# Sorting two entries of one layer per round, with the longest tile split by count

## The chip, the cores and the metric

The kernel runs on one core of a Trainium2 chip. The metric is the device time of one execution in microseconds, the median of several runs. A core has five engines that work through their own instruction streams side by side: TensorE (PE, matrix products), VectorE (DVE, elementwise work), ScalarE (ACT, functions and copies), GpSimd (POOL, which here issues the gathering DMAs) and SyncE (SP, which issues plain DMAs). They wait for each other through semaphores.

## What is computed

The input is a batch of 16 graphs of 1024 nodes, with 64 features per node and a sparse weighted adjacency matrix. Four layers follow each other. Layers 0 and 1 are products with the adjacency and small dense products. Layers 2 and 3 replace the sum over the neighbours by quantiles:

```
# layer 0: x = layernorm(x + tanh([x, adj @ x] @ W1 + b1) @ W2 + b2)
# layer 1: x = layernorm(x + (adj / max(rowsum(adj), 1)) @ x)
# layers 2 and 3, each with its own W1, b1, W2, b2:
adj_ = adjacency with ones on the diagonal
neigh = adj_ > 0, without the diagonal
# from a node with more than 10 neighbours every skip-th neighbour is taken out,
# skip = (neighbours + 1) // 2, and each taken edge goes in both directions
nd = adj_ after that > 0
s = sort(where(nd, x[neighbour], inf))       # per node and feature, over the neighbours
agg = sum over tau, w in (0.25, 0.25), (0.5, 0.5), (0.75, 0.25):
      w * (linear interpolation of s at tau * (count - 1))
x = layernorm(x + (relu((x + agg) @ W1 + b1) @ W2 + b2) * mask)
```

The set of valid neighbours is the same for layers 2 and 3, so a graph's lists are made once and used twice.

## The kernel before

**Words.** An entry is one of the 16 graphs. Below, "layer 0" and "layer 1" of the sorting are the reference's layers 2 and 3; this is also how the code counts them. A slot is one neighbour position of a list: 64 features (elements) for each of 128 rows.

**Preparing an entry.** `features` loads the adjacency in 128-column pieces, computes the first two layers, and keeps a 0/1 matrix of who is near whom. `lists` thins the neighbours, orders the rows of the graph by their count of neighbours, and writes for each ordered tile of 128 rows the list of neighbour indices (`idx`); VectorE's MAX8 finds them eight at a time. `ordered` brings features, masks and counts into the same order, and makes the interpolation weights. The lists of one entry are made after those of the one before.

**Tiles.** The 1024 ordered rows are 8 tiles of 128 rows, and tile t has at most `SIZES[t]` neighbours per row: 10, 11, 13, 14, 15, 17, 19 and 33. For the first seven, called the listed tiles here, GpSimd gathers the neighbours' features from a table in HBM: one indirect DMA for each slot but the first (L362), 92 for an entry and a layer, into a ring of 60 slots (`got_s`) that holds two entries side by side. For the tile of 33 slots, called the tail, no lists are made: TensorE picks the rows with one-hot matrices (`hot`), 24 products for each slot (L358), and ScalarE copies them out of PSUM (L742).

**Sorting.** A fixed network of min and max operations between strided views, alternating between the tile and a second buffer `other`, leaves the wanted order statistics in place (`exchange_plan`). Each min or max is one VectorE instruction for both entries of a pair at once (all VectorE calls of this part show line L207, a helper that counts their cost). `weigh` multiplies the wanted slots by their weights on ScalarE (L781) and adds them up on VectorE, into `agg`. `finish` runs the small dense network and the layernorm, and scatters the result rows with eight indirect DMAs (L826): to the second table after layer 0, to the output after layer 1.

**Rounds.** Round k sorts layer 0 of entry k and layer 1 of entry k - 2 side by side, for k = 0 to 17. Rounds 0 and 1 therefore have layer 0 alone, rounds 16 and 17 layer 1 alone, and each other round has a pair. In a round the tiles go from 19 slots down to 10, then the tail. `finish_round` of a round is done during the next.

**Order.** On VectorE, ScalarE and TensorE the order is written by the program itself: `Weave` keeps a clock of estimated VectorE time, and after each exchange it lets every other piece of work (a Python generator that yields how long its step takes) advance to that clock. `fetch` issues a tile's gathers as soon as the ring has a place and the entries are ready, in the order of `order_of_tiles`. `prepare` may start entries up to `allowed`, that is k + 2. GpSimd's and SyncE's DMAs are placed by a scheduler.

Of the kernel before, what the change touches and what calls it, by code (L numbers as in the profile page):

```python
# [12 lines left out]
F32 = mybir.dt.float32  # L13
# [8 lines left out]
P = 128  # L22
# [3 lines left out]
SIZES = (10, 11, 13, 14, 15, 17, 19, 33)  # L26
LEAST = (1,) + SIZES[:-1]
KS = -(-(max(SIZES[:-1]) - 1) // 8) * 8
KW = max(SIZES)
HOTS = 6  # L30
# [182 lines left out]
def adj_resnorm_kernel(ctx: ExitStack, tc: tile.TileContext, x, adj_t, nodemask, w01, b01, w02, b02,  # L213
# [3 lines left out]
    NT = N // P  # L217
    H = w21.shape[1]
# [42 lines left out]
    bounds = const.tile([1, 2 * NT], F32, name="bounds")  # L261
    for t in range(NT):
        nc.vector.memset(bounds[:, t : t + 1], float(SIZES[t]))
        nc.vector.memset(bounds[:, NT + t : NT + t + 1], float(LEAST[t]))
# [39 lines left out]
    want_ids = const.tile([P, NT, most_wanted], F16, name="want_ids")  # L304
# [6 lines left out]
    weights = const.tile([P, NT, most_wanted], F32, name="weights")  # L311
    mask_all = const.tile([P, B, NT], F32, name="mask_all")
    with tc.tile_pool(name="setup", bufs=1) as setup, \
# [11 lines left out]
        n1 = setup.tile([P, NT], F32, name="n1s")  # L325
        nc.vector.tensor_scalar(n1, nth.to_broadcast([P, NT]), -1.0, None, op0=ALU.add)
        hats(weights, [P, NT, most_wanted], n1, want_ids)
# [8 lines left out]
    table = [[dram.tile([N + 1, C], F32, name=f"table{layer}{i}") for i in range(3)] for layer in range(2)]  # L336
# [69 lines left out]
    def features(b, e):  # L406
# [72 lines left out]
        nc.sync.dma_start(table[0][b % 3][:N, :].rearrange("(t p) c -> p t c", p=P), x2)  # L479
        while b >= 2 and not entries[b - 2].filled[0]:  # L480
            yield 2
        parts = s.feat.tile([P, NT, 3, C], BF, name="x2p")
# [3 lines left out]
    def lists(b, e, pace):  # L486
# [103 lines left out]

        order = s.sets.tile([P, NT, N], BF, name="order", tag="takes")
# [7 lines left out]
        e.idx = s.feat.tile([P, NT, KS], I32, name="idx", bufs=5)  # L599
        pks, codes, found = {}, {}, []  # L600
        for t in (*reversed(range(NT)), -1, -2, -3):
# [19 lines left out]
            if 0 <= done < NT - 1:  # L621
                best = s.work.tile([P, KS], F16, name="best", bufs=1)
                less = s.work.tile([P, N], F16, name="less", bufs=1)
                rest, size = codes[done], -(-(SIZES[done] - 1) // 8) * 8
                for k in range(0, size, 8):
                    dve.max(best[:, k : k + 8], rest)
                    if k + 8 < size:
                        dve.match_replace(less, best[:, k : k + 8], rest, 0.0)
                        rest = less
                dve.tensor_scalar(e.idx[:, done, :size], best[:, :size], -1.0, float(N), op0=ALU.mult, op1=ALU.add)  # L630
        e.listed = True

    def ordered(b, e, order, own):
# [17 lines left out]
        e.rows = s.feat.tile([P, NT], I32, name="rows", bufs=6)  # L651
        dve.tensor_copy(e.rows, sorted_own[:, :, 1])
        e.out_rows = s.feat.tile([P, NT], I32, name="out_rows", bufs=6)
        dve.tensor_scalar(e.out_rows, sorted_own[:, :, 1], float(b * N), None, op0=ALU.add)
        e.mask = s.feat.tile([P, NT], F32, name="mask_s", bufs=6)
        dve.tensor_copy(e.mask, sorted_own[:, :, 2])
        yield 7
        while b >= 3 and entries[b - 3].xs[1] is None:
            yield 2
        e.xs[0] = s.feat.tile([P, NT, C], F32, name="x2s", bufs=3)  # L660
# [9 lines left out]
        while b >= 4 and not entries[b - 4].filled[1]:  # L670
            yield 2
        place = s.feat.tile([P, NT, P], F16, name="place", bufs=4)
# [12 lines left out]

        e.none = s.feat.tile([KW - 1, P], BF, name="none", bufs=5)
        wts = s.feat.tile([P, NT, most_wanted], F32, name="wts", bufs=5)
        for h in range(NH):
# [11 lines left out]
            for q in range(G):  # L700
                nc.tensor.matmul(pw[:, q, :], counted[:, q, :], weights[:KW, h * G + q, :], start=True, stop=True)
            yield 9
            nc.scalar.copy(wts[:, half, :], pw)
# [9 lines left out]
        nc.tensor.transpose(pc[:1, :NT], ends[:, P - 1 : P], ident[:NT, :NT])  # L713
        nc.tensor.transpose(pc[:1, NT : 2 * NT], ends[:, 0:1], ident[:NT, :NT])
        yield 7
        mf = s.work.tile([1, 2 * NT + 1], F32, name="mf", bufs=1)
        nc.scalar.copy(mf[:, : 2 * NT], pc[:1, : 2 * NT])
        yield 5
        dve.tensor_sub(mf[:, : 2 * NT], mf[:, : 2 * NT], bounds)
        dve.tensor_scalar(mf[:, NT : 2 * NT], mf[:, NT : 2 * NT], -1.0, None, op0=ALU.mult)  # L720
        dve.reduce_max(mf[:, 2 * NT :], mf[:, : 2 * NT], axis=AX.X)
        dve.tensor_copy(over[:, b : b + 1], mf[:, 2 * NT :])

    def members(k):

        return [(m, b, entries[b]) for m, b in enumerate((k, k - 2)) if 0 <= b < B]

    def fill(k):

        while k and (k - 1, NT - 1) not in free:  # L730
            yield 1
        t = NT - 1
        size = SIZES[t]
        got = tails[k] = s.lists.tile([P, 2, size, C], F32, name="got", tag="got_l", bufs=1)
        for m, b, e in members(k):
            while e.parts[m] is None or e.xs[m] is None or e.place is None or e.none is None:
                yield 1
            nc.scalar.copy(got[:, m, 0, :], e.xs[m][:, t, :])
            waiting = None

            def empty():
                nc.scalar.copy(got[:, m, waiting[0] : waiting[0] + 4, :], waiting[1])  # L742

            for i in range(1, size):
# [13 lines left out]
                whole = i < LEAST[t]  # L758
# [3 lines left out]
                pick(pg[:, i - first, :], hot, e.parts[m], whole)  # L762
# [8 lines left out]
            e.filled[m] = True  # L771

    def weigh(k, t, got, agg, which):

        want = wants[t]
        while any(e.wts is None for m, b, e in members(k)):
            yield 1
        prods = got[:, :, : len(want), :]
        for i, slot_id in enumerate(want):
            for m, b, e in members(k):  # L780
                nc.scalar.activation(prods[:, m, i, :], got[:, m, slot_id, :], AF.Copy, scale=e.wts[:, t, i : i + 1])  # L781
            if i % 6 == 5:
                yield 3
        yield 13
        left = len(want)
        while left > 2:
            more = left // 2
            dve.tensor_add(prods[:, which, :more, :], prods[:, which, :more, :], prods[:, which, left - more : left, :])
            left -= more
        dve.tensor_add(agg[:, which, t, :], prods[:, which, 0, :], prods[:, which, 1, :])  # L790
        free.add((k, t))

    def finish(b, e, layer, agg):
# [3 lines left out]
        y = s.work.tile([P, NT, C], F32, name="y_m", bufs=1)  # L797
        dve.tensor_add(agg, agg, xc)
        yield 2
        for h in range(NH):  # L800
            pt = s.psum.tile([P, HALF], F32, name="pt", tag="m", bufs=1)
# [3 lines left out]
            o_t = s.work.tile([C, HALF], F32, name="o_t", bufs=1)  # L805
            nc.scalar.copy(o_t, pt[:C])
            yield 3
            ph = s.psum.tile([P, HALF], F32, name="ph", tag="m", bufs=1)
            nc.tensor.matmul(ph[:H], w1s, o_t, start=True, stop=True)  # L809
            yield 7  # L810
            h_t = s.work.tile([H, HALF], F32, name="h_t", tag="o_t", bufs=1)
            nc.scalar.activation(h_t, ph[:H], AF.Relu, bias=b1c)
            yield 3
            pd = s.psum.tile([P, G, C], F32, name="pd", tag="m", bufs=1)
# [6 lines left out]
        xn = agg if layer else s.feat.tile([P, NT, C], F32, name="x3s", bufs=3)  # L821
        yield from settle(xn, y, "m")
        yield 1
        dst, rows = (out_rows_of, e.out_rows) if layer else (table[1][b % 3], e.rows)
# [10 lines left out]
    def read_back(b, e, src):  # L835

        while b and not entries[b - 1].filled[1]:
            yield 2
# [3 lines left out]
        parts = s.feat.tile([P, NT, 3, C], BF, name="x3p", bufs=1)  # L842
# [3 lines left out]
    class Weave:  # L846
# [34 lines left out]
        def finish(self, gen):  # L881
            while self.runs(gen):
# [3 lines left out]
                               wts=None, parts=[None, None], xs=[None, None], filled=[False, False]) for _ in range(B)]  # L886
# [4 lines left out]
    order_of_tiles = [(k, t) for k in range(B + 2) for t in reversed(range(NT - 1))]  # L891
# [16 lines left out]
    def fetch(must=-1):  # L908

        while len(gots) < len(order_of_tiles):  # L910
            n = len(gots)
            k, t = order_of_tiles[n]
            first = room[0] if room[0] + SIZES[t] <= ROOM else 0
            taken = [i for i in holders[first : first + SIZES[t]] if i is not None and order_of_tiles[i] not in free]
            there = [e.xs[1] is not None if m else ready(b) for m, b, e in members(k)]
# [6 lines left out]
            for m, b, e in members(k):  # L922
                while not (e.xs[1] is not None if m else ready(b)):
                    weave.advance()
                nc.scalar.copy(got[:, m, 0, :], e.xs[m][:, t, :])
                for i in range(1, SIZES[t]):
                    gather(got[:, m, i, :], table[m][b % 3], e.idx[:, t, i - 1 : i])
            gots.append(got)

    def finish_round(k, agg, sums):  # L930
# [3 lines left out]
        for m, b, e in members(k):  # L934
            yield from finish(b, e, m, agg[:, m])

    def sort_round(k):
# [4 lines left out]
        first = members(k)[0][0]  # L942
        which = slice(first, first + len(members(k)))
        agg = s.feat.tile([P, 2, NT, C], F32, name="agg")
        sums = []
        for t in (*reversed(range(NT - 1)), NT - 1):
            if t == NT - 1:
                weave.finish(filling)
                got = tails[k]
            else:  # L950
                n = order_of_tiles.index((k, t))
                fetch(n)
                got = gots[n]
            other = s.lists.tile([P, 2, SIZES[t], C], F32, name="other", bufs=1)
            pair = got[:, which], other[:, which]
            for is_max, d, v, i, j, to in usual[t]:
# [319 lines left out]
```

## Time and profile before

| what | value |
|---|---|
| median of 3 runs | 5177.79 us (5170.74 to 5182.22) |
| span of the profiled execution | 5178.8 us |
| exchanges and sums `TENSOR_TENSOR` on VectorE, a pair's round (rounds 3 to 13) | 306 instructions on `got`, `got_s` and `other` |
| one-hot picks on TensorE (L358) | 24,576 |
| gathers (L362) | 2944, 3320.8 us, mean 1128 ns |
| scatters (L826) | 256 |
| products on ScalarE (L781), listed tiles | 1568, mean 336 ns |
| copies of picked rows on ScalarE (L742) | 256, mean 369 ns |
| VectorE MAX8 with 1024 inputs | 240, 1.2 us each |

The rounds end at these times of the span: 476, 719, 1047, 1344, 1640, 1936, 2231, 2525, 2821, 3117, 3413, 3709, 4004, 4300, 4561, 4841, 4964 and 5142 us. Rounds 16 and 17, with one entry each, last 123 and 178 us; 37 us follow for the last entry's network and output.

A page's row says for a group of instructions: line, engine, operation, output and input with shape, how many, then busy time and mean duration, then the engine's idle time just before them and what ended it. An engine's busy share is a mean over the whole span. Time in which an engine issues a DMA or waits for a semaphore is not counted as busy.

### The profile page before, as it was taken

The page shows a single profiled execution, that of the slowest core. Times are in us where ns is not written, and L with a number is a line of the kernel's source. Part 1 is how long each engine was busy: PE and PEld are TensorE (multiplying, and loading weights), DVE is VectorE, ACT ScalarE, POOL GpSimd, SP SyncE. Part 2 cuts the span into 40 slices and gives each one's busy share as a digit, 9 for nine tenths or more (in the row PEclk, how much of TensorE's full clock was granted, in tenths as well). Part 3 has the DMA queues.
Part 4 walks back from the last instruction along what each step waited for, and adds up shares of the span by engine and source line. Part 5 has one row for each costly group of instructions (what it writes and reads, how often), then busy time and mean ns, then how long its engine had stood idle before and what let it go on. Part 6 is the DMA issues. An engine that isn't in the chain of part 4 may idle for free. (4 is left out here: it accounts for less than half of the span.)

```text
span 5178.8 us, 109085 instructions
## 1 busy us (share of the span) xinstructions
PE 3420.0 (66%) x43512; PEld 2622.0 (51%) x43512; DVE 4472.1 (86%) x8771; ACT 2755.6 (53%) x6304; POOL 3632.1 (70%) x3229
## 2 busy tenths in 40 slices
PE   6878777486775848687685858677584857343432
PEld 5656656264564726465563636466463645233321
DVE  2488788889899898989989898989989899977976
ACT  3465474565556565565557555565656546233332
POOL 0336574777778787777777787777778787877572
PEclk7887878697877968787787878787796877555555
DMA  3222222122221312222221222222121111111010
GB/s 86 74 54 64 65 57 54 38 59 61 56 62 40 73 42 48 59 57 63 51 65 41 59 46 53 61 56 62 43 73 42 43 45 25 23 24 25 16 26 10
DMA packets 420598, 259.24 MB, mean 50 GB/s; under 512 B 106590, under 2 KB 368878, under 8 KB 420078
## 3 DMA queue, kind: packets, MB, share of 16 engines
q0 software_dynamic: 102400, 105.06, 10.5%
q1 hardware_dynamic: 317678, 147.12, 10.2%
q8 instruction: 342, 5.60, 0.5%
q14 instruction: 178, 1.46, 0.1%
HBM read 239.37 MB, written 12.58 MB: 49 GB/s over the span
## 5 line engine op out<-in xcount | busy, mean ns | idle before, releaser
L362 POOL DMA_INDIRECT got_s<-table,idx x2944 | 3320.8, 1128 | 1358.9 <-issue 675.0
L358 PEld LDWEIGHTS <-hot 128*128 128x128 bf16 x24576 | 961.9, 109 | 843.4 <-DVE hot L207 661.0
L358 PE MATMUL pgk<-x3p,hot 128*128 128x64 bf16 x12288 | 554.2, 213 | 363.1 <-DVE hot L207 328.0
L358 PE MATMUL pgk<-x2p,hot 128*128 128x64 bf16 x12288 | 512.6, 206 | 324.6 <-DVE hot L207 286.3
L520 PE MATMUL pr<-steps,near 128*128 128x512 bf16 x1536 | 421.6, 440 | 288.4 <-ACT junk L526 183.1
L207 DVE TENSOR_TENSOR other<-got_s 128x512 f32<-128x512 f32 (+8 forms) x900 | 512.4, 583 | 102.9 <-DMA got_s<-table,idx 79.6
L781 ACT ACTIVATE got_s<-got_s,wts 128x64 f32<-128x64 f32 x1568 | 399.6, 336 | 236.6 <-DVE got_s L207 235.2
L207 DVE TENSOR_TENSOR got_s<-got_s 128x384 f32<-128x384 f32 (+6 forms) x918 | 491.8, 538 | 19.7
L607 PE MATMUL pk<-near,order 128*128 128x512 f16 x2048 | 473.2, 386 | 0.0
L742 ACT COPY got<-pgk 128x256 f32<-128x256 f32 x256 | 94.5, 369 | 695.0 <-PE pgk L358 686.2
L564 PE MATMUL pv<-minus_n,takes 128*128 128x128 bf16 x1024 | 243.5, 262 | 300.5 <-DVE takes L207 299.9
L520 PEld LDWEIGHTS <-near 128*128 128x128 f16 x1536 | 166.8, 110 | 533.3 <-issue 406.9
L207 DVE TENSOR_TENSOR got_s<-other 128x512 f32<-128x512 f32 (+8 forms) x774 | 407.1, 539 | 7.8
L465 PE MATMUL pa<-x,adj_r 128*128 128x65 f32 x2048 | 348.7, 343 | 64.6 <-ACT x L388 24.6
L207 DVE TENSOR_SCALAR hot<-place 128x1024 bf16<-128x1024 f16 x768 | 343.7, 452 | 37.4 <-PE pgk L358 37.0
L564 PEld LDWEIGHTS <-takes 128*128 128x128 bf16 x1024 | 119.6, 117 | 501.5 <-DVE takes L207 331.1
L465 PEld LDWEIGHTS pa<-x,adj_r 128*128 128x128 f32 x2048 | 335.3, 257 | 67.4 <-ACT x L388 25.3
L563 PE MATMUL pv<-scaled,near 128*128 128x128 f16 x1024 | 244.9, 263 | 166.4 <-ACT near L568 165.2
L207 DVE TENSOR_TENSOR other<-other 128x128 f32<-128x128 f32 (+13 forms) x558 | 320.5, 574 | 15.9
L607 PEld LDWEIGHTS <-order 128*128 128x128 bf16 x2048 | 196.5, 100 | 227.9 <-issue 18.0
L526 ACT ACTIVATE junk<-pr,nb_st 128x1024 f16<-128x1024 f32 x256 | 282.0, 1108 | 51.5 <-PE pr L520 51.2
L752 ACT ACTIVATE hot<-far,one_f 128x1024 bf16<-128x1024 f16 x256 | 294.0, 1148 | 8.4
(202 smaller groups left out, 7196.9 us busy)
## 6 DMA issues: line engine op xcount, KB each, us to landing
adj_r<-in_adj_dram SPq DMA_DIRECT2D x256, 512.0 KB
got_s<-table,idx POOLq DMA_INDIRECT x2944
x_s<-in_x_dram SPq DMA_DIRECT2D x16, 256.0 KB
table<-x SPq DMA_DIRECT2D x16, 256.0 KB
x<-table SPq DMA_DIRECT2D x16, 256.0 KB
table<-x3s,rows POOLq DMA_INDIRECT x128
out_dram<-agg,out_rows POOLq DMA_INDIRECT x128
table<-no_row SPq DMA_DIRECT2D x6, 0.2 KB
```

The source lines that it names most:

```text
L207: return call(*args, **kwargs)
L358: nc.tensor.matmul(dst, hot[:, c, :], parts[:, c, q, :], start=first and c + q == 0, stop=c == NT - 1 and q == 2)
L362: nc.gpsimd.indirect_dma_start(out=dst, out_offset=None, in_=tab, in_offset=bass.IndirectOffsetOnAxis(ap=rows, axis=0))
L465: nc.tensor.matmul(pa[:, q, :], adj[i][:, jt, :], x1[:, jt, :], start=jt == 0, stop=jt == NT - 1)
L520: nc.tensor.matmul(pr[:, h * HALF : (h + 1) * HALF], near[:, c, t * P : (t + 1) * P], steps[:, ONSET + h * HALF - c * P :][:, :HALF], star ...
L526: nc.scalar.activation(junk, prs[t - 1], AF.Sign, bias=lim[:, i, t - 1 : t], scale=-1.0, accum_out=cut_at[:, i, t - 1 : t])
L563: nc.tensor.matmul(pv[:, cols], near[:, c, rows], scaled[:, c, :], start=True, stop=False)
L564: nc.tensor.matmul(pv[:, cols], takes[:, c, rows], minus_n, start=False, stop=False)
L607: nc.tensor.matmul(cols, order[:, c, t * P : (t + 1) * P], left(c, slice(h * G, (h + 1) * G)), start=c == 0, stop=c == NT - 1)
L742: nc.scalar.copy(got[:, m, waiting[0] : waiting[0] + 4, :], waiting[1])
L752: nc.scalar.activation(by_act, far, AF.Relu, bias=one_f, scale=-1.0)
L781: nc.scalar.activation(prods[:, m, i, :], got[:, m, slot_id, :], AF.Copy, scale=e.wts[:, t, i : i + 1])
```

## The change

A round now sorts two neighbouring entries of the same layer: `members` takes the pair from `order_of_rounds`, which is (0,0), (0,1), (1,0), (0,2), (1,1), (0,3), ..., (1,5), (0,7), (1,6), (1,7), each a layer and a pair of entries. These are 16 rounds. In round 0 the listed tiles go one entry at a time (`present`), since the second entry is not ready then.

The tail is split. Of its 128 rows, sorted by count, the lower 64 need 21 slots at most and the upper 64 need 33. An odd entry has the two halves of its last tile swapped, so that the lower half of one entry and the upper half of the other, 64 rows each, make one tile of 128 rows: a tile with 21 slots and one with 33 for a pair, in place of two with 33. A product of `weigh` for the tail then serves both entries at once. The picks by TensorE are as before, and go to the halves by two copies in place of one.

More entries are under way: six tables per layer in place of three, more buffers for lists, weights and features, and `allowed` is k + 4. A round's gathers are issued when both entries are there. Of the last round, the networks of both entries run side by side on buffers of their own.

```diff
-SIZES = (10, 11, 13, 14, 15, 17, 19, 33)
-LEAST = (1,) + SIZES[:-1]
+SIZES = (10, 11, 13, 14, 15, 17, 19, 21, 33)
+LEAST = (1,) + SIZES[:7] + (20,)
+LISTED = 7
+TABLES = 6
...
+    def halves_of(b):
+        return (7, 8) if b % 2 == 0 else (8, 7)
...
+        if b % 2:
+            for least, shift in ((N - P, P // 2), (N - P // 2, -P)):
+                dve.tensor_scalar(key[:, 3], key[:, 1], float(2 * least - N + 1), float(shift), op0=ALU.is_ge,
+                                  op1=ALU.mult)
+                dve.tensor_add(key[:, 2], key[:, 2], key[:, 3])
...
     def members(k):
-        return [(m, b, entries[b]) for m, b in enumerate((k, k - 2)) if 0 <= b < B]
+        layer, pair = order_of_rounds[k]
+        return layer, [(m, 2 * pair + m, entries[2 * pair + m]) for m in range(2)]
...
+            at = [(rows, (0, short)[plan - LISTED], SIZES[plan]) for rows, plan in zip((lower, upper), halves_of(b))]
...
             def empty():
-                nc.scalar.copy(got[:, m, waiting[0] : waiting[0] + 4, :], waiting[1])
+                for rows, off, most in at:
+                    if waiting[0] < most:
+                        nc.scalar.copy(got[rows, off + waiting[0] : off + waiting[0] + 4, :], waiting[1][rows])
...
+        if t >= LISTED:
+            wts = members(k)[1][0][2].ends
+            prods = got[:, : len(want), :]
+            for i, slot_id in enumerate(want):
+                nc.scalar.activation(prods[:, i, :], got[:, slot_id, :], AF.Copy, scale=wts[:, t - LISTED, i : i + 1])
...
+    order_of_rounds = [(0, 0), (0, 1)]
+    for pair in range(2, B // 2):
+        order_of_rounds += [(1, pair - 2), (0, pair)]
+    order_of_rounds += [(1, B // 2 - 2), (1, B // 2 - 1)]
+    tasks = []
+    for k in range(len(order_of_rounds)):
+        for present in ((0,), (1,)) if k == 0 else ((0, 1),):
+            tasks += [(k, t, present) for t in reversed(range(LISTED))]
...
-            there = [e.xs[1] is not None if m else ready(b) for m, b, e in members(k)]
+            there = [e.xs[1] is not None if layer else ready(b) for m, b, e in both if m in present]
             if n > must and (taken or not all(there)):
                 return
...
+        weave.finish(filling)
+        for t in range(LISTED, NS):
+            off = sum(SIZES[LISTED:t])
+            got = tails[k][:, off : off + SIZES[t], :]
+            other = s.lists.tile([P, WIDE, C], F32, name="other", bufs=1)
+            exchange(t, (got, other[:, : SIZES[t], :]), cut)
+            summed(t, got, None, (0, 1))
...
-        for k in range(B + 2):
-            allowed[0] = k + 2
+        for k in range(len(order_of_rounds)):
+            allowed[0] = k + 4
             sort_round(k)
```

## The prediction

> **What bounds the kernel now.** I read first the busy shares and the slices, then the span cut at the round ends (a round ends where VectorE writes the last `agg<-got`), then the GpSimd timeline, the groups by form, and the waits.
>
> ```profile
> PE 3420.0 (66%) x43512; PEld 2622.0 (51%) x43512; DVE 4472.1 (86%) x8771; ACT 2755.6 (53%) x6304; POOL 3632.1 (70%) x3229
> ...
> DVE  2488788889899898989989898989989899977976
> ...
> POOL 0336574777778787777777787777778787877572
> ```
>
> VectorE (DVE) leads, with dips at both ends. GpSimd (POOL) looks 30% free. It is not, as the next two views show. The span by rounds (columns: window, its length, then PE, PEld, DVE, ACT, POOL busy with counts):
>
> ```profile
> 0.00:476.00 476.00, 374.05 (x3422) 280.23 (x3423) 283.83 (x745) 231.04 (x470) 161.56 (x178) 0.81 0.28 72
> ...
> 3709.00:4004.00 295.00, 202.60 (x2719) 151.90 (x2719) 273.47 (x505) 171.81 (x394) 227.65 (x200) 0.81 0.23 55
> ...
> 4561.00:4841.00 280.00, 98.99 (x1620) 85.00 (x1620) 216.00 (x408) 95.27 (x257) 210.26 (x186) 0.57 0.12 24
> 4841.00:4964.00 123.00, 62.99 (x830) 50.66 (x830) 106.58 (x292) 46.10 (x119) 62.83 (x58) 0.53 0.09 19
> 4964.00:5179.00 215.00, 67.04 (x847) 53.68 (x846) 136.31 (x366) 60.86 (x165) 97.72 (x100) 0.52 0.08 16
> ```
>
> Rounds 3 to 13 all look like the second line: 295.5 us with 273.5 of VectorE (idle 22) and 200 indirect DMAs on GpSimd. The GpSimd timeline shows what one costs:
>
> ```profile
> 3969.07 1.70 POOL L826 DMA_INDIRECT out_dram<-agg,out_rows  x1 [0.30 <-issue]
> 3971.08 1.36 POOL L826 DMA_INDIRECT out_dram<-agg,out_rows  x1 [0.30 <-issue]
> 3972.74 1.37 POOL L362 DMA_INDIRECT got_s<-table,idx  x1 [0.30 <-issue]
> ...
> 3977.56 0.94 POOL L362 DMA_INDIRECT got_s<-table,idx  x1 [0.30 <-issue]
> 3978.81 0.94 POOL L362 DMA_INDIRECT got_s<-table,idx  x1 [0.30 <-issue]
> ```
>
> A DMA occupies 0.94 us at least, and 0.305 always follow before the next: that gap is GpSimd's own time. So 200 of them take 227.65 + 61 = 289 of 295.5 us. **Two engines are full at once**: VectorE with its stalls and GpSimd at 98%. GpSimd runs some 96 gathers ahead, as far as the ring of 60 slots lets it, so VectorE sets the pace by a little. In round 15 (4561 to 4841) VectorE has only 216 us and the round still lasts 280: there GpSimd rules (186 x 1.435 = 267). The line 3969.97 of VectorE's timeline explains the 1.70 and 1.36 above:
>
> ```profile
> 3969.97 1.62 DVE L207 TENSOR_TENSOR other<-got 128x1408 f32<-128x1408 f32 x1
> 3971.63 1.62 DVE L207 TENSOR_TENSOR got<-got 128x1408 f32<-128x1408 f32 x1
> ```
>
> The DMA started at 3971.08 ends at 3972.44, the DMA before it at 3970.77; both began while a long exchange ran, and neither took the 0.94. Costs of exchanges, by form:
>
> ```profile
> L207 DVE TENSOR_TENSOR got_s<-other 128x512 f32<-128x512 f32 x270 | 179.6, 686 | 2.6
> ...
> L207 DVE TENSOR_TENSOR got<-other 128x1024 f32<-128x1024 f32 x98 | 117.1, 1217 | 0.0
> ...
> L207 DVE TENSOR_TENSOR other<-got 128x2048 f32<-128x2048 f32 x14 | 32.1, 2291 | 0.4
> ```
>
> So an exchange takes 0.155 us + 1.042 ns per element. Last, the waits, and the writing of entry 3's index list:
>
> ```profile
> DVE other L207 <- DMA got_s<-table,idx: 79.6, 9, 18.7
> ```
>
> ```profile
> 776.80 0.18 DVE L207 TENSOR_SCALAR idx<-best 128x24 int32<-128x24 f16 x1
> ...
> 824.98 0.17 DVE L207 TENSOR_SCALAR idx<-best 128x16 int32<-128x16 f16 x1
> ```
>
> VectorE waits little for gathers today (80 us in all). Lists come out at 217, 416, 614 and 825 us for entries 0 to 3, one per 200 us: nothing of an entry can be gathered before.
>
> **What the Trainium skill says.** "SBUF — State Buffer", section "Who interferes with whom": an exchange with two SBUF inputs takes the read port that VectorE and GpSimd share, and whoever comes second is blocked until the other ends and the same section reports that such exchanges were not seen to stall DMAs that GpSimd issues. This trace differs, and decides: gathers that start with VectorE idle take 0.946 us on average (285 of them), those that start inside a 512-element exchange 1.15 (535), inside a 2048-element one 2.17 (28). "VectorE: DVE Perf Modes", section "The TRN2 errata", says that each instruction pays a fixed time whatever its size; here 0.155 us.
>
> **The change, part by part.** From the two orders of instructions:
>
> *Exchanges.* Tiles of 10 to 19 slots need 222 exchanges over 706 slots, the 33-slot tile 66 over 384, the new 21-slot tile 49 over 188; the sums of products are 21 instructions over 42 slots, 5 over 20, and 10 over 28 for the two new tails (their last add is two). A slot is 64 elements, twice that where two entries lie side by side. Before: 18 rounds x 314 = 5652 instructions, 32 x 1152 x 64 = 2.359 M elements: 876 + 2458 = 3334 us. After: a round has 222 + 21 + 49 + 66 + 10 = 368; 16 of them, and 243 more because round 0 takes its listed tiles one entry at a time: 6131 instructions, 2.146 M elements: 950 + 2236 = 3187. **VectorE -148 us**, of which a pair's round has 202.3 -> 196.8 = -5.5; the rest is in the four one-entry rounds that go. Added: four 0.19 us instructions for each odd entry, 6 us. On the path in rounds 1 to 11.
>
> *GpSimd.* Still 2944 gathers and 256 scatters. But no exchange is over 1024 elements any more. A gather is held up with a chance that goes with an exchange's duration d, and for a time that goes with d, so the mean delay goes with the sum of d² over the round: 176 before, 127 after (us², from the orders). Delay before 1.138 - 0.945 = 0.193; the same rule gives 1.14 and 1.08 for rounds 15 and 16, and the windows have 1.13 and 1.08. After: 0.945 + 0.142 = 1.087, with the gap **1.39 us per DMA**, 278 us per round, against 289.
>
> *ACT.* Products of the tail: 32 x 21 become 16 x 28, 224 fewer at 0.336 = -75; the copies of picked rows go by halves, 160 more. A 64-partition copy is not in the trace: at most the 0.369 of the 128-partition row (59 us), at least nearly nothing; I take 0.369. ACT is 53% busy; it hides either way, and uncovered would cost 3 us a round. PE: the 24,576 picks stay. Ring, buffers and more tables cost nothing.
>
> *Waits added.* Gathers of a round are issued only when both entries are there. That is two lists for a layer-0 round, two finishes for a layer-1 round; behind a waiting gather stand all later gathers and scatters on GpSimd's queue, and VectorE waits for them. By the order, the finish matters only for rounds 2 and 15 (elsewhere it lies three rounds back).
>
> **The sum.** *Start.* Round 0 sorts entries 0 and 1 alone, and its tail; round 1 needs entry 3's list. Less exchange work lies beside that list than now, so I put its end at 788 (now 825; unloaded, entry 0's list took 135 us from its adjacency, loaded 178). VectorE has then 244 of 292 us of round 1 left by the order; in these units a steady round now is 280 and takes 295.5, factor 1.056: round 1 ends at 1045. *Middle.* Rounds 2 to 11 hold 2796: 2952 us, plus 15 for gathers that start late in rounds 3 and 5, whose second list is finished 42 us into the round and 31 before its end: 4010. Per round 291 against 295.5; GpSimd's 278 fits. *End.* Rounds 12 to 15 prepare less or nothing, VectorE needs 264 and then 221, GpSimd 200 x 1.395 = 279: GpSimd rules. At 4010 it is 96 gathers ahead; up to round 14's last it has 456 gathers and 40 scatters: 692, at 4702. Round 15 needs round 13's second finish, which stands behind round 14's last listed tile on VectorE: 40 us idle, 13 for the scatter and its landing, then 184 gathers and 8 scatters, 267: 5022. Behind the last gather the 10-slot exchange, two tails, products and finish: 117 (today 100 with one tail). Sum 5139; I say **5135**. That is against the profiled 5178.8, a microsecond over the median of 5177.8.
>
> So of 148 us saved some 45 arrive: the end, which was two one-entry rounds of 123 and 178 us, becomes two pair rounds that GpSimd limits.
>
> **Rivals.** (A) The above, 5090 to 5180, chance 0.50. (B) The end is cheaper, because the gathers shrink to their floor when VectorE idles there: the 496 and 192 DMAs at 1.25 us are 620 and 240, so 4010 + 620 + 40 + 13 + 240 + 117 = 5040. For: round 17 had gathers of 0.99. Against: in round 15, with VectorE 77% busy, the mean was 1.13. Chance 0.17. (C) Slower: GpSimd's lead is lost at the both-entries wait. Where a second list comes at or after the end of the round ahead, VectorE finds nothing gathered, and waits for 36 gathers, 50 us, half covered by other work: 25 a time. In three of the layer-0 rounds 5, 7, 9, 11, 13 that is 75, so 5210. It decides from the point where the second list comes within 50 us of its round. For: by the order it comes after round 3 has begun, and 31 us before round 5. Against: 67 to 118 us before the later ones. Chance 0.28. (D) The parts cancel (GpSimd was the only bound and keeps its 289): 5175. Chance 0.05.
>
> **How the numbers follow.** A measurement of this kernel can tell some 0.2%, 10 us, from no change. Faster: 0.42 of A and all of B, 0.59. Same: 0.06 of A and 0.04 of D, 0.10. Slower: C and what is left, 0.31. The range runs from B to C: 5045 to 5215. A alone has 5090 to 5180.
>
> **What would show it.** Right: steady rounds of 288 to 293 us; gathers of 1.08 to 1.10 on average there; entry 3's list near 788; rounds 13 to 15 near 280 each with VectorE under 80% busy, waiting for gathers. Wrong: `DVE other <- DMA got_s` waits of 20 us or more at the start of every layer-0 round (C), or last rounds near 230 (B).

## The result and the profile after

| | before | after |
|---|---|---|
| median | 5174.26 us (5168.96 to 5182.22) | 5301.43 us (5293.2 to 5311.65) |
| ratio after to before, 95% interval | | 1.0246, 1.0226 to 1.0267 |
| span of the profiled execution | 5178.8 us | 5291.5 us |

The changed kernel is 2.5% slower, where 0.8% faster was forecast. Five runs, named near the end of the experiments, were taken while the kernel before itself took 6928 to 7132 us, and can only be set against each other. The page's busy shares and slices of the kernel after:

```profile
PE 3412.4 (64%) x43576; PEld 2637.1 (50%) x43576; DVE 4296.5 (81%) x9266; ACT 2809.6 (53%) x6314; POOL 3467.3 (66%) x3296
...
DVE  2577848798788989897987987799899999596775
...
POOL 0435327757477776767677674776767777777771
```

VectorE has 176 us less to do than before and GpSimd 165 less, and yet the span is 113 longer. So neither of the two fullest engines got more work: both wait more. The granted clock, the mean share of its full speed that TensorE was given, is 0.745 for 0.756 before; it is not the reason, since `ring70` and `places_readback` below take 95 and 112 us less at 0.746 and 0.748. The sixteen rounds end at 680, 1081, 1367, 1746, 2039, 2338, 2648, 2962, 3288, 3594, 3888, 4172, 4431, 4703, 4997 and 5238 us. Some of them by windows (window, length, then PE, PEld, DVE, ACT and POOL busy):

```profile
680.00:1081.00 401.00, 247.86 (x3050) 185.61 (x3051) 285.84 (x596) 208.98 (x449) 254.54 (x235) 0.76 0.21 53
...
1367.00:1746.00 379.00, 257.45 (x3198) 196.49 (x3194) 313.37 (x630) 190.99 (x430) 267.04 (x246) 0.78 0.20 50
...
2962.00:3288.00 326.00, 229.10 (x2759) 171.97 (x2759) 267.55 (x568) 182.98 (x411) 214.20 (x200) 0.75 0.21 51
...
4431.00:4703.00 272.00, 98.43 (x1620) 84.23 (x1620) 209.42 (x437) 95.92 (x250) 211.97 (x198) 0.58 0.12 26
```

Take the third line, round 8. VectorE is busy 267.55 us of 326, six less than in a steady round before (273.5 of 295.5). GpSimd's 200 DMAs take 214.20 + 200 x 0.305 = 275 of the 326. Before, they took 289 of 295.5. Each engine has grown lighter and the round longer. What VectorE waits for, over the whole span:

```profile
DVE other L211 <- DMA got_s<-table,idx: 363.2, 29, 26.4
DVE hot L211 <- PE pgk L374: 56.5, 27, 5.1
...
DVE near L211 <- DMA adj_r<-in_adj_dram: 35.8, 7, 22.9
```

The wait for gathers has gone from 79.6 us to 363.2. And GpSimd, which issues them, waits for VectorE at the same time: rounds 5 to 11 of the kernel after, then seven steady rounds of the kernel before, by what GpSimd waited for:

```profile
POOL got_s L378 <- DVE other L211: 182.1, 40, 50.8
```

```profile
POOL got_s L362 <- DVE other L207: 23.0, 35, 5.5
```

These are waits for a place in the ring: an exchange that writes `other` reads the slots that the gather will overwrite. So in one and the same round VectorE stands for want of gathers, and GpSimd for want of room. One round shows where. Below is a steady round before and round 6 after, each cut at the start of the tail (columns as above):

```profile
2231.00:2431.00 200.00, 164.72 (x2403) 131.01 (x2404) 182.03 (x380) 110.69 (x263) 153.87 (x146) 0.83 0.26 62
2431.00:2525.00 94.00, 43.05 (x316) 29.53 (x315) 91.96 (x127) 61.20 (x132) 75.45 (x56) 0.70 0.18 40
```

```profile
2338.00:2523.00 185.00, 131.12 (x2094) 104.90 (x2094) 152.04 (x341) 139.95 (x295) 135.28 (x123) 0.83 0.20 48
2523.00:2648.00 125.00, 79.83 (x703) 62.00 (x701) 118.07 (x235) 39.59 (x117) 84.10 (x78) 0.67 0.24 65
```

Before, VectorE's listed part of the round is 182 us of work in 200, and GpSimd puts 146 DMAs beside it. After, it is 152 us of work in 185: 33 us stand still there. What left it is the MAX8 search for a list, 30 us. VectorE's instructions on `best`, which are this search, lie in the listed part of the round before and in the tail of round 6 after:

```profile
2231.00:2431.00 200.00, 30.32 (x38) 0.83 0.26 62
2431.00:2525.00 94.00, 0.00 (x0) 0.70 0.18 40
```

```profile
2338.00:2523.00 185.00, 0.00 (x0) 0.83 0.20 48
2523.00:2648.00 125.00, 29.91 (x38) 0.67 0.24 65
```

Before, the search begins 52 to 57 us into every round from 2 to 14. After, it begins 217, 209, 202, 189, 163, 157 and 135 us into rounds 4 to 10: in rounds 4 to 6 wholly in the tail, in rounds 7 to 10 in part or wholly ahead of it, but late. What GpSimd must still bring for the listed part has not become less with it, as is worked out below. The waits themselves, on VectorE's and on GpSimd's timeline (the last bracket is the idle time ahead and what ended it):

```profile
2447.32 0.82 DVE L211 TENSOR_TENSOR other<-got_s 128x640 f32<-128x640 f32 x1 [3.98 <-DMA got_s<-table,idx]
2488.35 0.56 DVE L211 TENSOR_TENSOR other<-got_s 128x384 f32<-128x384 f32 x1 [21.84 <-DMA got_s<-table,idx]
...
2659.31 1.89 POOL L378 DMA_INDIRECT got_s<-table,idx  x1 [28.75 <-DVE other L211]
```

The waiting exchange at 2488.35 is the first of the 10-slot tile, the last gathered one of the round. The same exchange waits in every round from 2 to 10, of layer 0 and of layer 1 alike, for 8 to 26 us, and in rounds 4 to 9 the wait ends 144 to 152 us after the round's start. This can be worked out from the ring. `fetch` puts a tile to place 0 when what is left is too small; 19 + 17 + 15 slots make 51, the 14-slot tile doesn't fit into the 9 that remain, and so the ring holds three tiles: 48 gathers for each entry, 96 for two. When a round starts, 96 of its 184 gathers are done and the ring is full. The rest, 88 gathers and 8 scatters, start some 11 us into the round, when the first tile has been read, and take 96 x 1.39 = 133 us: the last lands near +145, however soon VectorE gets there. Before, the search lay ahead of that tile, and VectorE was not early. In rounds 4 to 10 it lies behind the exchange that waits. VectorE is early and waits, comes in round 6 to a tail that has grown to 125 us, and there GpSimd fills the ring and stands.

Round 8 has a second thing, on the timelines of SyncE, GpSimd and VectorE:

```profile
3182.47 4.02 SPq L433 DMA_DIRECT2D adj_r<-in_adj_dram  x2
3223.93 0.37 SPq L902 DMA_DIRECT2D x<-table  x1
3224.46 9.20 SPq L433 DMA_DIRECT2D adj_r<-in_adj_dram  x4
...
3212.74 1.00 POOL L888 DMA_INDIRECT table<-x3s,rows  x1 [0.30 <-DMA got_s<-table,idx]
...
3221.71 0.97 POOL L888 DMA_INDIRECT table<-x3s,rows  x1 [0.30 <-issue]
...
3229.57 0.69 DVE L211 TENSOR_SCALAR near<-adj_r 128x1024 f16<-128x1024 f32 x1 [22.94 <-DMA adj_r<-in_adj_dram]
```

`read_back` (L902) reads an entry's x3 from the table once its eight scatters have landed. The scatters stand behind gathers in GpSimd's queue and end at 3222.7. SyncE issues the read only at 3223.93, and the adjacency loads of the next entry, which need nothing of x3, stand behind the read. The Trainium skill, page "DMA: Bandwidth & Descriptors", section "Anatomy of one DMA — SWDGE (gpsimd) path", says that DMA engines do not wait on semaphores and that any such wait takes place on the sequencer that issues the DMA. The section describes DMAs from GpSimd; on SyncE this trace agrees, with 41 us from the start of one issue to the next. VectorE lost 22.9 us there.

### The profile page after: what moved, and what is told of

Its sections match the earlier page's. It is cut to its first block, busy times and chain, and to the rows that moved or that the text cites. A ratio compares the mean times of both kernels' runs of the same rounds, so it can differ in the third digit from the quotient of the medians.

```text
span 5291.5 us, 109614 instructions
## 1 busy us (share of the span) xinstructions
PE 3412.4 (64%) x43576; PEld 2637.1 (50%) x43576; DVE 4296.5 (81%) x9266; ACT 2809.6 (53%) x6314; POOL 3467.3 (66%) x3296
## 5 line engine op out<-in xcount | busy, mean ns | idle before, releaser
L378 POOL DMA_INDIRECT got_s<-table,idx x2944 | 3172.8, 1078 | 1634.3 <-issue 594.8
L211 DVE TENSOR_TENSOR other<-got_s 128x512 f32<-128x512 f32 (+9 forms) x850 | 508.2, 609 | 390.7 <-DMA got_s<-table,idx 363.2
L780 ACT COPY got<-pgk 64x256 f32<-64x256 f32 x416 | 151.9, 365 | 670.3 <-PE pgk L374 667.0
L211 DVE TENSOR_TENSOR got_s<-got_s 128x128 f32<-128x128 f32 (+9 forms) x867 | 481.9, 559 | 19.5 <-ACT got_s L829 1.7
L481 PE MATMUL pa<-x,adj_r 128*128 128x65 f32 x2048 | 387.6, 372 | 135.0 <-ACT x L404 58.1
L481 PEld LDWEIGHTS pa<-x,adj_r 128*128 128x128 f32 x2048 | 377.2, 287 | 142.8 <-ACT x L404 60.1
L211 DVE TENSOR_TENSOR got_s<-other 128x512 f32<-128x512 f32 (+9 forms) x731 | 402.0, 563 | 7.5
L211 DVE TENSOR_SCALAR hot<-place 128x1024 bf16<-128x1024 f16 x768 | 329.1, 434 | 56.5 <-PE pgk L374 56.5
L211 DVE TENSOR_TENSOR other<-other 128x384 f32<-128x384 f32 (+10 forms) x617 | 323.7, 525 | 17.3
L211 DVE MAX8 best<-code 128x8 f16<-128x1024 f16 x240 | 293.8, 1224 | 45.9 <-ACT code L639 40.8
L788 ACT ACTIVATE far<-place,minus_k 128x1024 f16<-128x1024 f16 x256 | 292.8, 1144 | 6.2 <-DVE place L211 4.4
```

Of the source, the lines that this page charges most:

```text
L211: return call(*args, **kwargs)
L378: nc.gpsimd.indirect_dma_start(out=dst, out_offset=None, in_=tab, in_offset=bass.IndirectOffsetOnAxis(ap=rows, axis=0))
L481: nc.tensor.matmul(pa[:, q, :], adj[i][:, jt, :], x1[:, jt, :], start=jt == 0, stop=jt == NT - 1)
L780: nc.scalar.copy(got[rows, off + waiting[0] : off + waiting[0] + 4, :], waiting[1][rows])
L788: nc.scalar.activation(far, e.place, AF.Abs, bias=minus_k[:, i + 2 : i + 3])
```

## The experiments

Edits are to the changed kernel unless the text says otherwise. The theory tested is that the ring's room and the order of DMAs in the queues let the two engines wait in turns (the ring theory). Its rivals: GpSimd is too slow as such (its rate), the lists come too late, the split is what costs.

**The ring.** A longer ring needs memory, which fewer one-hot buffers give. So there are two kernels, `hots3` as control and `ring70`, in which four tiles (65 slots, 122 gathers) fit.

```diff
-HOTS = 6
+HOTS = 3
-ROOM = 60
+ROOM = 70      # ring70 alone
```

> The changed kernel with 3 buffers for the one-hot matrices in place of 6: the control for the run with a larger ring, which needs their room. Both theories: TensorE gets its one-hot matrices later, 5300 to 5340.

> As the run with 3 one-hot buffers, with a ring of 70 slots in place of 60: four tiles (65 slots, 122 gathers) can be gathered ahead during a tail stage, not three (51 slots, 96 gathers). Theory L (the ring is full in the tail stage): GpSimd's waits for a free place at the round ends go, VectorE's waits for gathers in rounds 5 to 9 too, 80 to 120 us less than the control. Rival G: no change against the control.

Measured: 5351.14 us for the control (ratio to before 1.0333, 1.0306 to 1.036), a little more than was expected, and 5206.06 with the longer ring (1.0058, 1.0037 to 1.0079): 145 us less for ten slots. VectorE's waits, control first:

```profile
DVE other L211 <- DMA got_s<-table,idx: 300.9, 25, 27.7
DVE hot L211 <- PE pgk L374: 271.2, 142, 7.4
```

```profile
DVE hot L211 <- PE pgk L374: 298.5, 158, 7.4
DVE other L211 <- DMA got_s<-table,idx: 92.7, 6, 37.5
```

The gathers are as many and as long; only how far they may run ahead differs. VectorE's waits for them fall by 208 us, and none over 2 us is left in rounds 2 to 12. GpSimd's waits for room fall too, but only to half, from 312.6 to 157.6 us. GpSimd's rate alone falls as the cause in these rounds. Of the 137 us between the two spans, 84 lie in rounds 2 to 11, 21 before and 32 behind them. The waits for `pgk` are the price of fewer one-hot buffers, in both.

**The same ring, filled.** The order of the listed tiles and their places are fixed so that the 60 slots hold four tiles (19, 17, 13, 11), 112 gathers for a pair.

```diff
+ORDER = (6, 5, 2, 1, 4, 3, 0)
+PLACES = {6: 0, 5: 19, 2: 36, 1: 49, 4: 0, 3: 19, 0: 36}
-            tasks += [(k, t, present) for t in reversed(range(LISTED))]
+            tasks += [(k, t, present) for t in ORDER]
-            first = room[0] if room[0] + SIZES[t] <= ROOM else 0
+            first = PLACES[t]
```

> The changed kernel with the same ring of 60 slots and all its buffers, but each tile at a fixed place and the tiles in the order 19, 17, 13, 11, 15, 14, 10 slots: the first four fill the 60 slots (112 gathers ahead of a round; in the changed kernel three tiles of 51 slots, 96 gathers, and 9 slots lie idle), so 72 gathers are left for the listed stage, not 88. Ring theory (GpSimd stands still with a full ring in the tail stage, and VectorE then waits for the last gathers of the listed stage): 16 gathers of 1.39 us are 22 us per round, nearly all of the 15 to 30 us of waiting in rounds 5 to 9; 5200 to 5230. Rival (GpSimd's own rate sets the rounds, however many slots there are): 5300.

Measured: 5262.53 us (1.0174, 1.0154 to 1.0195), 39 less than after, where 70 to 100 less was expected. Rounds 5 to 7 last 289, 301 and 300 us, for 299, 310 and 314; the waits for gathers fall from 363.2 to 190.3. But rounds 8 and 10 now last 349 and 325, with the other wait of round 8 (the edit adds two lines, so that L211 is L213 here):

```profile
DVE other L213 <- DMA got_s<-table,idx: 190.3, 19, 46.9
...
DVE near L213 <- DMA adj_r<-in_adj_dram: 83.2, 8, 59.3
```

More gathers ahead would mean that a scatter stands behind more of them, that x3 is read later, and that SyncE's queue stands longer; the next edit tests this.

**The read of x3 on GpSimd's queue.** There it waits behind its own scatters, and SyncE is free.

```diff
-        nc.sync.dma_start(x3, src[:N, :].rearrange("(t p) c -> p t c", p=P))
+        nc.gpsimd.dma_start(x3, src[:N, :].rearrange("(t p) c -> p t c", p=P))
```

> The changed kernel with the read of the second table (x3) issued by GpSimd, behind the scatters that it waits for, and not by SyncE. Theory S (in the changed kernel SyncE's queue waits at this read for scatters that stand behind gathers on GpSimd, the adjacency loads behind it come late, and VectorE stops at them in the tail stage, 23 us in round 8, while the ring is full): that wait goes, round 8 falls from 326 to about 300, the whole by 20 to 40 us to about 5270. Against: each read costs GpSimd about 1.3 us and perhaps the landing of the scatters, 2 us, 16 times, at most 50 us in all; if GpSimd's rate is the bound, 5300 to 5350.

Measured: 5286.44 us (1.0227, 1.021 to 1.0244); round 8 goes from 326 to 301. The place was right. The total gives back 15 us, less than the 20 to 40 that were expected, and its interval overlaps that of the kernel after, so that in the total the gain is not clear of noise. 373.5 us of waits for gathers are still there.

> The fixed places (5262) with the read of x3 issued by GpSimd. Theory S: the waits of 59 us and less for the adjacency in rounds 8 and 10 (349 and 325 us) go, both rounds fall to about 300, the whole to 5180 to 5200. Rival (they are the ring's): no change, 5260.

With both edits: **5189.68 us** (1.004, 1.0026 to 1.0054), as expected. Rounds 8 and 10 fall from 349 and 325 to 303 and 300. The two edits alone gave 39 and 15, together they give 112: `places` alone leaves 83.2 us of waits for the adjacency, `readback` alone 373.5 for gathers, both together 15.1 and 178.6.

**Lists earlier, lists later.** If the search belongs into the listed part, moving it should do what the ring does. `lists_early` gives the preparation a pace of 0.7 (a smaller number runs further ahead) and begins entry b's list no sooner than the tail of round b - 4; `lists_late` keeps the pace and holds the search for entry b until the tail of round b - 3. In both, `tailing[0]` is the round whose tail has begun.

```diff
+            while b >= 4 and b > tailing[0] + 4:      # lists_early
+                yield 2
+            pace = 0.6 if b < 4 else 0.7
...
+        while b >= 6 and b > tailing[0] + 3:          # lists_late
+            yield 2
```

> The changed kernel with the making of an entry's list paced faster (0.7 in place of 1.0 from entry 4 on) and held until the tail stage of the round four before, so that the search for neighbours (MAX8) lies in the middle of the listed tiles in rounds 4 to 12 (in the changed kernel it lies in the tail stage in rounds 4 to 7 and just before it in 8 to 12). Theory L (the search was the work that let GpSimd catch up with the 88 gathers that follow the opening of the ring; moved into the tail stage, VectorE waits for gathers in the listed stage and GpSimd waits for the ring in the tail stage): VectorE's idle time in rounds 4 to 9 falls from 25-59 us to about 20, the rounds to 284-291, the whole to about 5180 (ratio to before about 1.00). Rival G (the wait for both entries, or GpSimd's own rate, sets the rounds): no change within 0.5%, 5300.

> The changed kernel with the search for neighbours held back to the tail stage of the round three before it is needed, in all rounds from 4 to 12 (in the changed kernel it comes forward again from round 8 on). Theory L: rounds 9 to 12, now 306, 294, 284 and 258 us, become like rounds 5 to 7 (300 to 314), VectorE waiting some 15 to 25 us for gathers in each; the whole rises by 40 to 70 us to about 5350. Rival G: no change, 5300.

Measured: 5260.76 us early (1.0164, 1.0143 to 1.0186) and 5305.42 late (1.0265, 1.0234 to 1.0296). Early: 5180 was expected, 5300 by the rival, and the result lies between. The search begins 35 to 39 us into rounds 5 to 11, and these last 2054 us together, for 2133: 79 less, near the forecast for them (2037). But 21 us are lost in rounds 0 to 4 and 27 behind round 11, most of them in round 12. VectorE's wait for `code` in the search grows from 40.8 to 123.9 us, by 23 us in rounds 0 to 4 and by 57 in rounds 5 to 11. Late: rounds 10 to 12 get longer by 7, 23 and 30 us, as the ring theory has it. But the adjacency wait of round 8 is gone (326 to 304 us), round 13 is 20 us shorter, and the sum is that of the kernel after, which is what the rival had. So the ring theory is right here in the rounds alone, and misses the sum.

**The split taken away.** The lower half also has 33 slots, so that a pair has two tails of 33 as before; the ring then has 51 slots, all used, hence again three tiles.

```diff
-SIZES = (10, 11, 13, 14, 15, 17, 19, 21, 33)
+SIZES = (10, 11, 13, 14, 15, 17, 19, 33, 33)
-ROOM = 60
+ROOM = 51
```

> The changed kernel with the lower half's tail at 33 slots too, that is without the split by count (ring of 51 slots to make room, which holds the same three tiles at the same places): 17 exchanges and 196 slots more per round, 15.7 us of VectorE. If the tail stage is on the path (GpSimd stands still in it with a full ring): 13 rounds of 15.7 and part of the last three, 200 to 240 us more, 5500 to 5540. If GpSimd's rate sets the rounds: 5300 to 5350.

Measured: 5379.04 us (1.0394, 1.0374 to 1.0415). VectorE has 262 us more to do (4558.6) and the kernel takes 78 longer; the waits for gathers fall from 363.2 to 197.4, and rounds 7 to 11 take 1519 us, for 1524 in the kernel after. This is under the 5500 to 5540 that were expected and over the 5300 to 5350 of GpSimd's rate. In sum the split is worth 1.5%, where its work is 5%. But the run does not test the split alone: the search begins 117, 90, 61 and 50 us into rounds 6 to 9, ahead of the exchange that waited, and with the same three tiles in the ring no wait for gathers over 2 us is left in rounds 6 to 12. What the split would be worth with the search held in place is not shown. The pairing without the split costs 3.9%.

**The start.** Round 1 also takes its listed tiles one entry at a time, so that entry 2 need not wait for entry 3's list.

```diff
-        for present in ((0,), (1,)) if k == 0 else ((0, 1),):
+        for present in ((0,), (1,)) if k <= 1 else ((0, 1),):
```

> The changed kernel with the listed tiles of round 1 taken one entry at a time, as those of round 0. Theory (the wait for entry 3's list: GpSimd stands still 124 us before it with entry 2's tiles half fetched, and VectorE then waits 100 us in round 1): round 1 ends 30 to 45 us earlier although VectorE has 243 instructions more (37 us), 5260 to 5275. Rival (the start is set by the lists alone and not by the pairing): the 37 us come on top, 5335.

Measured: 5381.15 us (1.0402, 1.0369 to 1.0435), 80 longer, where 35 less was expected. Round 1 ends at 1102, not sooner (1081), and rounds 3, 8 and 10 take 396, 347 and 327 us, with 57.1 us of waits for the adjacency. GpSimd no longer stands 123.8 us until entry 3's list comes, but it stands 46.6 and 52.3 us for room in the ring at the end of round 0 and of round 1. Taking away the wait of both entries for each other thus does not shorten round 1; whether the ring took what it gave is not shown.

Two kernels put edits together:

> The fixed places, the lists begun earlier (pace 0.8 from entry 4 on) and round 1 one entry at a time, together. Ring theory with the other two: rounds 4 to 11 at 285 to 290 us, round 1 shorter by 40: 5110 to 5160, under the kernel before. Rival (GpSimd's rate): 5260 at best.

> Fixed places, the read of x3 on GpSimd, and the lists begun earlier with pace 0.8 (as in the run of the three mended parts, without the one-entry round 1, which cost 80). Ring theory with S: rounds 4 to 11 at 285 to 295, 5110 to 5160, at or under the kernel before (5174). Rival (GpSimd's rate): 5200 or more.

They took 5241.02 us (1.0118, 1.009 to 1.0147; `places`, `single1` and early lists at a pace of 0.8) and 5231.69 (1.0123, 1.0106 to 1.014; `places`, `readback` and the same lists). Both miss the 5110 to 5160 of the ring theory, and the second lies where the rival had it. Once the ring is mended, the earlier lists lengthen rounds 2 to 6 together (by 41 us in the second, against `places_readback`), `code` again being waited for (96.9 us in all, 15 of them more in these rounds).

**The kernel before with the filled ring.** The same fixed places, in the kernel before.

> The kernel before with the fixed places alone (112 gathers ahead in place of 96). Ring theory: in the kernel before GpSimd had 6 us of long waits per round and VectorE none for gathers in rounds 3 to 13, so the ring does not limit it: within 0.5% of before. If the larger lead helps any kernel of this kind: 20 to 40 us less than before.

Measured: **5147.05 us** (0.9951, 0.9934 to 0.9967), faster than the kernels before and after, and the least time of all here. Both expectations held it, as their ranges overlap. The gain is not in the steady rounds, which last 291 to 306 us and 19 us more together. It is at the ends: rounds 0 to 2 are 18 us shorter, and rounds 15 and 17, where GpSimd rules, go from 280 to 259 and from 178 to 166.

**The moved read in the kernel before.** Is SyncE's standing queue new with the change?

> The kernel before with the fixed places and with the read of x3 taken from SyncE's queue to GpSimd's. In the kernel before VectorE waited 22.7 us in all for the adjacency (7 times), and 25.4 us (8 times) with the places. If SyncE's queue standing at x3 is a cost that the change brought with it, the read is worth nothing here: 5135 to 5160, within 0.3% of 5147 of before_places. If the standing queue is as dear in any order of rounds, 60 us or more should go, as with the changed kernel (5262.53 to 5189.68): 5075 to 5090.

> The same kernel as before_places_readback, which ran on a chip where the kernel before itself took 7098.52 us, so that its 1.016 says nothing of the others' 5174 us. Expected as there: within 0.3% of before_places (ratio 0.992 to 0.998 to the kernel before) if SyncE's queue standing at x3 is a cost that the change brought with it; ratio 0.98 to 0.985 if it is as dear in any order of rounds.

> The same kernel as before_places, beside the next run on one chip, so that the two are set against each other whatever this chip's pace: ratio 0.995 to the kernel before at the usual pace (5170 us for the kernel before).

> The kernel before with the fixed places and the read of x3 on GpSimd's queue, beside before_places_again. If SyncE's queue standing at x3 is a cost that the change brought: within 0.3% of before_places_again. If it is as dear in any order of rounds: 1.2% or more below it.

> As before_places_readback_3, if the chip is back at its usual pace (some 5170 us for the kernel before): 5135 to 5160 if SyncE's queue standing at x3 is a cost that the change brought; 5075 to 5090 if it is as dear in any order of rounds.

Side by side on one chip, 7219.75 us without the move and 7257.28 with it: no gain that can be told. The ratios to the kernel before with the move are 1.016, 1.019, 1.0202 and 1.0227, without it 1.018. But here VectorE is busy 62% of the span and GpSimd 48% (`before_places_again`), and VectorE has no wait for gathers, so that neither engine is near full and these five runs cannot answer the question. The traces of the earlier runs give a hint: in `before_places` VectorE waits 25.4 us in all for the adjacency, at most 6.6 at a time, against 83.2 and 59.3 in `places`. An experiment that settles it is missing, and the gain of `before_places` is shown only beside a kernel before of 5170 us.

## Why the prediction was wrong

By its own sum, 5139 us against a span of 5291.5: the start is 36 longer (round 1 ends at 1081, not 1045), rounds 2 to 11 take 3091 us for 2965, 126 longer, and the end 1119 for 1129, 10 shorter. (The terms 1045, 2952 and 15 make 4012 and not 4010, a slip of 2 us; and the gathers of round 17 before, which it has at 0.99 us for (B), take 73.69 / 76 = 0.97.)

- *Exchanges.* Right in the main: -148 + 6 forecast, -176 measured for all of VectorE; what the other 34 us are is open.
- *GpSimd.* Right: 1.087 us for a gather in a steady round was forecast, and in rounds 5 to 11 the mean is 1.088 (1.134 before). Over the whole span it is 1078 ns, for 1128:

```profile
L378 POOL DMA_INDIRECT got_s<-table,idx x2944 | 3172.8, 1078 | 1634.3 <-issue 594.8
...
L780 ACT COPY got<-pgk 64x256 f32<-64x256 f32 x416 | 151.9, 365 | 670.3 <-PE pgk L374 667.0
```

- *ACT.* The 365 ns of a half copy is the 0.369 that was taken. ScalarE's total rose by 54 us where the two terms made -16. That it hides at 53% is not borne out in full: in rounds 5 to 11 VectorE waits 37.9 us in all for ScalarE, where it waited 5.7 before, and in `places_readback` 91.1. Whether the copies are the reason was not tried.
- *Start.* Entry 3's list came at 792, forecast 788. Round 1 still lasted 401 us: VectorE has 285.84 us of work in it and 115 of idle time, where the sum took a factor of 1.056 from steady rounds. The ring starts empty there, and waits of 11.4 and 26.4 us for gathers fall into it. Taking away the wait of both entries did not shorten it (`single1`). What makes up the 36 us, and the 379 of round 3, in which VectorE has the searches of two lists (313.37 us of work), is open. With ring and read mended the two rounds still last 406 and 372.
- *Middle: the step that failed*, "Per round 291 against 295.5; GpSimd's 278 fits". It compares each engine's sum over a round with the round. Both sums were right, and rounds 5 to 11 still took 299 to 326 us but for the last two (294, 284). A round is two stages, and the ring carries at most 96 gathers from the one into the other. The list search moved from the listed stage into the tail, or to the end of the listed stage behind the last gathers, so that VectorE is early for the last listed tile and GpSimd later has no room. "GpSimd runs some 96 gathers ahead" stood in the prediction as a cushion; it was the limit. `ring70` against `hots3` shows this (-145 us in all, 84 of the spans' 137 in rounds 2 to 11), and `lists_early` that it is about the place of the search (rounds 5 to 11 at 2054). A second part, SyncE's queue, wasn't in the sum at all: -73 us, once the ring is filled (`places` to `places_readback`). Both edits together take the 5301.43 down to 5189.68, 112 of the 127 us by which the kernel after is slower than the one before. In the traces they bring back 88 of the middle's 126 us; the other 38 are open, and the longer waits for ScalarE are a candidate that no run tests.
- *End.* Right in sum: VectorE is busy 209.42 of 272 us in round 13 and waits for gathers, as it does in rounds 14 and 15. These rounds were forecast near 280 each and last 272, 294 and 241.
- *Rivals.* (C) had the right sign and named the right wait, but not its place: it put it at the start of layer-0 rounds for want of a second list. After round 3 the wait stands mostly at the last listed tile, in rounds of both layers. (B) is refuted by the end, where a DMA of round 13 still takes 211.97 / 198 = 1.07 us and not the floor of 0.945, and (D) by GpSimd's 275 of 326.

What stays open: the start, what is left in the middle, and why earlier lists cost so much in the first rounds and at the end. In no version tried does the pairing by layer beat the kernel before; the best is 0.4% above it.

## What to carry to other kernels

When two engines are both near full, do not add each one's work over a loop and compare it with the loop: cut the loop into its stages, and check for each that what the buffer between them can carry covers the difference. When a change moves work from one stage to another, count what the buffer really holds (here 51 of 60 slots, since a tile is never split), and where a plain read waits for a scatter, look for what stands behind it on its queue. Filling the buffer made both kernels faster, by 0.7% and 0.5%.

## What the runs showed of the hardware

The delay of gathers by exchanges goes with the exchanges' length: no exchange over 1024 elements is left, and the mean gather of rounds 5 to 11 fell from 1134 to 1088 ns, where the rule by squared durations, taken from the kernel before, gave 1087. A ScalarE copy of 256 elements on 64 partitions takes 365 ns, one on 128 partitions 369: half the rows saved nothing.
